# Moving lists, routing and layer-norm steps within the order of a gated attention and mixture-of-experts layer

## The chip, the cores and the metric

The kernel runs on one core of one Trainium2 chip. Its time is the device time of one execution in microseconds (us). A profile is taken from one execution by the hardware profiler; all instants are us from the start of its span. The engines are PE (matrix multiply, with its weight loads PEld), DVE (vector), ACT (scalar functions), POOL (general, here also the engine that issues indirect DMAs) and SP (which issues the other DMAs in the order of its queue).

## The reference

x is 8 batches of 512 tokens of 256 numbers, float32.

```python
x = x + tanh(g_xattn[0]) * xattn(layernorm(x), ctx, ctx, mask, ...)   # 16 heads of 16
x = x + tanh(g_ffn[0]) * ffn(layernorm(x), ...)

# ffn: 8 experts of 256 -> 1024 -> 256, two for each token
probs = softmax(x_flat @ router_w + router_b)
top_w, top_idx = top_k(probs, 2)
for e in range(8):
    out += comb[:, e:e+1] * (gelu(x_flat @ expert_up[e].T) @ expert_down[e].T)
```

All of this is computed in float32. Each of the 8 experts has 2 MB of weights. The mask is the same for all queries and heads and leaves a short run of keys, and the kernel finds that out on the chip and branches on it.

## The kernel before

**Ahead of the branch** (to about 19 us) the kernel loads the mask, the weights and x of batch 0, takes the statistics of batch 0's rows, finds the window of keys from the mask, and computes from it the flag `near_i` (L609), on which all engines branch (L1587). `measure` (L211) makes the layer norm's numbers: `look` runs BN_STATS and the aggregate for four tiles of 128 rows (L225, L228), and `settle` twelve small DVE operations that end in the scale and the shift (L233 to L246). Between the flag and the branch stand on DVE `drop` (L611, which reads the bank `row_ps` of a PE product), `pick`, `bks` and three `keep_ones` (L619). x of batch 1 is loaded behind the window load (L516), which waits on SP for the first key.

**Inside the branch** (`attend_near`) the attention of eight batches runs as one software pipeline. The outer loop's iteration b goes from -1 to 7. Each iteration has four groups g (a half c of the heads and an index i), and each group three slots n. A group of iteration b issues the attention weights of batch b (`weights_T`: `w_ps`, four products on PE with exponentials on ACT, L1058 and L1063), the product with the values of the group before (`weigh`: `n_av` on PE, then `raw`, its reciprocal, and `oT` on DVE, L1076 to L1090), the scores of batch b+1 (`find_tops`: `t_ps` on PE, the row maxima `tops` on DVE, L1028 and L1033), and `lower_tops` (`top_ps` on PE, `ql` on DVE, L1046 and L1047). All else is put in a plan of 12 places (g, n) by `between(old, new, next_)` with old = b-1, new = b+2 and next_ = b+3:

- for the new batch: keys and values (`kv_ps`, L539), `keys_T` (`k_ps`, with four ACT copies to `k`, L551 and L557), `keys_less` (`km`), the scales of its normalized rows (`xn_a` on ACT, L275), their transposes (`xnT_ps_a`, L285) and the two `queries` (`q_ps`, L570)
- for the next batch: the look and settle of its rows
- for the old batch: `project_out` in two halves (`proj_ps`, added to x on DVE, L1102), look and settle, the scales `xn_f`, the transposes, `logits` (`route_ps`), and then, one iteration later, the routing: `route` (a transpose `lg_ps`, L332, and some twenty small DVE operations with one exponential on ACT, which choose two experts for each token), `place` (`place_ps` on PE, `counts` on ACT, then POOL operations, which give each token a line in its expert's part of a table), and four steps `enter` of two indirect DMAs each, which write the table's entries (L398). `add_bias` runs on POOL for 2.35 us.

The banks of PSUM limit this order. The pool of scores has 5 banks, of which `t_ps` and `w_ps` take 4 each time; the pool "g" has 2, which `proj_ps`, `top_ps`, `lg_ps`, `kv_ps`, `k_ps`, `xnT_ps`, `q_ps`, `route_ps` and `place_ps` use in turn. PE takes its instructions in order, so it stands still where the next one's bank has not been read.

**The experts.** Tokens of one expert form groups of 256 (pairs) or 384 (triples). Of the 32 main groups 0 to 4 are planned when the first three batches are in the table (`plan_full(0)`), 5 to 16 when six are (`plan_full(1)`), and the others at the end (`plan_rest`). A group s needs its list of lines (`list_rows`, L806: SP reads the line number and loads 3 KB from the table), its rows (`fetch`, indirect DMAs on POOL, L826), its weights (`load`, L816 and L817, 1 MB each, three buffers), and then two products with GELU between them (L874, L892) and a scatter (L898). Groups 0 to 3 run between the attention groups of iterations 5 to 7 (the dictionary `amid`). From group 4 on `compute(s)` gives the steps of a group: fetch of s+2, the products, the turning of the next group's rows, the list of s+4, and the load of s+2. One step of the attention's last routing follows each of them: batches 6 and 7 are put into the table while groups 4 to 7 run. A list reads the table, so it waits for all entries that are issued ahead of it, and an entry waits for the reads ahead of it:

```python
            if s + 4 < end:
                steps.append(lambda: list_rows(s + 4))
            if s + 2 < end:
                steps.append(lambda: load(s + 2))
```

A framework puts the instructions of each engine in order by priority (that of the program) and by when its own model has the inputs ready, so an operation may slip ahead into a gap; `tc.keep_in_program_order` pins one to its place.

Of the kernel before, what the change touches and what calls it, by code (L numbers as in the profile page):

```python
# [68 lines left out]
def flamingo_layer(ctx: ExitStack, tc: tile.TileContext, a: dict, out: bass.AP):  # L69
# [190 lines left out]
    def shared(p2, small, bank):  # L260
        def layernorms(jobs, pin=False, measured=None):


            said, looks, settle_all = measured or measure(small, [job[:2] for job in jobs], pin)
            settle = lambda pin=False: settle_all(pin)

            def own(k):
                b, which, dst = jobs[k]

                def scale(ts):  # L270
                    if ts[0] == 0:
                        said[k] = p2.tile([P, QT, D], F32, tag="xn", name=f"xn_{which}_{b}")
                    for t in ts:
                        at = k * QT + t
                        ins = nc.scalar.activation(  # L275
                            said[k][:, t, :], xs[b][:, t, :], AF.Identity,
                            bias=said["shift"][:, at : at + 1], scale=said["rstd"][:, at : at + 1],
                        )
                        if t == ts[0] and pin:
                            tc.keep_in_program_order(ins)  # L280

                def turn(c):
                    ps = bank(f"xnT_ps_{which}_{b}_{c}")
                    for t in range(QT):
                        nc.tensor.transpose(ps[:, t * P : (t + 1) * P], said[k][:, t, c * P : (c + 1) * P], ident)  # L285
# [15 lines left out]
        def finish(b):  # L301
# [28 lines left out]
            def route():  # L330
                ps = bank(f"lg_ps{b}")[:, :P]
                nc.tensor.transpose(ps, said["lgT"], ident)  # L332
                lg = t3("lg")
                nc.vector.tensor_tensor(
                    lg, ps.rearrange("p (t e) -> p t e", t=QT)[:, :, :E], over_t(rb), ALU.add
                )
                mx = t2("mx")
                nc.vector.tensor_reduce(mx, lg, AX.X, ALU.max)
                nc.vector.tensor_tensor(lg, lg, over_e(mx), ALU.subtract)
                pr = t3("pr")  # L340
                nc.scalar.activation(pr, lg, AF.Exp)
                sm = t2("sm")
                nc.vector.tensor_reduce(sm, pr, AX.X, ALU.add)
                rs = t2("rs")
# [14 lines left out]
                both = t3("both")  # L359
                nc.vector.tensor_tensor(both, picks[:, :, 0, :], picks[:, :, 1, :], ALU.add)  # L360
                said["top"], said["picks"], said["both"] = top, picks, both
# [43 lines left out]
            return x2T, keep_x, keep_rows, logits, route, places  # L405

        return layernorms, finish

# [40 lines left out]
    with early, tc.tile_pool(name="ps_mask", bufs=1, space=PSUM) as ps_mask:  # L449
# [21 lines left out]
            ins = nc.vector.tensor_scalar(dropped[:, t, :], mask_i[:, t, :], 0.0, None, ALU.is_equal)  # L471
            tc.keep_in_program_order(ins)

        norms_0 = measure(const, [(0, "a")], True)
        settle_0 = norms_0[2]
        norms_0[1][0]()
        for t in range(QT):
# [35 lines left out]
            return t  # L513

        win = load_window(mk, 0)
        load_x(1, pin=True)  # L516
        wins = {1: load_window(const, 1, pin=True)}
        for dst, src in (
            (gates[:, 0:1], a["g_xattn"].partition_broadcast(P)),
# [87 lines left out]
        nc.vector.scalar_tensor_tensor(near, end, 1.0, near, ALU.is_ge, ALU.mult)  # L607
        nc.vector.scalar_tensor_tensor(near, uneven, 0.0, near, ALU.is_le, ALU.mult)
        tc.keep_in_program_order(nc.vector.tensor_copy(near_i, near))  # L609
        drop = column("drop", P)  # L610
        tc.keep_in_program_order(nc.vector.tensor_scalar(drop, row_ps, -1.0, 1.0, ALU.mult, ALU.add))  # L611
        nc.vector.scalar_tensor_tensor(pick, drop, lead, diag, ALU.mult, ALU.add)
# [6 lines left out]
            tc.keep_in_program_order(nc.vector.tensor_scalar(t[:, :, DH:], t[:, :, DH:], kept, None, ALU.mult))  # L619

        keep_ones(vals[0])
        for t in vals[1:]:
            keep_ones(t)
        for step in (keys_values, keys_T, lambda: stay_awake(6), keys_less):
# [4 lines left out]
    def experts(pool, seen, half_bank, bank, row_bank):  # L629
# [338 lines left out]
    def attend_near(att):  # L968
# [134 lines left out]

        normal = {}

        def normalize(*jobs):
            looks, settle, each = layernorms(jobs, True)
            for job, own in zip(jobs, each):
                normal[job[:2]] = own
            return looks, settle  # L1110

        def between(old, new, next_):
# [5 lines left out]
            def put(g, n, *steps):  # L1118
                plan[g, n] += steps

            jobs = []
            if old is not None:
                x2T, keep_x, keep_rows, logits, route, place = finish(old)
                jobs.append((old, "f", x2T))
            if next_ is not None:
                xnT[next_] = None
# [3 lines left out]
            if new is not None:  # L1130
# [18 lines left out]
                if new > 1:  # L1149
                    put(3, 0, bias)  # L1150
            if next_ is not None:
                put(*((2, 2) if old is None else (0, 2)), looks[-1])
            if old is not None:
                rows_f, scales, turns = normal[old, "f"]
                put(0, 1, lambda: project_out(old, (0, 1)))
                put(1, 0, lambda: project_out(old, (2, 3)), keep_x)
                put(1, 1, looks[0])
            if jobs:
                put(*((3, 1) if old is None else (1, 2)), settle)
            if old is not None:  # L1160
# [6 lines left out]
                later.append((route, place, enter, counts))  # L1167
            return plan


        def begin():
# [24 lines left out]
        DONE = 4  # L1196


        xnT, later = {}, deque()
        looks, settle = normalize((1, "a", lambda: xnT[1]))  # L1200
        for step in (*looks, settle):
            step()
        behind = None
        for b in range(-1, B):
            if b + 3 < B:
# [9 lines left out]
            if b == 0:  # L1215
                plan[0, 0] += looks
                plan[0, 1].insert(0, settle)
            for route, place, enter, counts in behind_route:
                plan[0, 2].append(route)
                plan[1, 2].append(place)  # L1220
                if counts:
                    plan[1, 2] += enter + counts
                else:
                    for where, step in zip(((1, 2), (2, 0), (2, 1), (2, 2)), enter):
                        plan[where].append(step)
            for g in range(4):
                c, i = g // 2, g % 2
# [20 lines left out]
        (route, place, enter, _), (route_last, last, enter_last, counts) = later  # L1248
        mixed = [step for pair in zip(rest, [route, place, *enter] + [wait] * len(rest)) for step in pair]
        spread = [step for one in enter_last for step in (one, wait, wait)]  # L1250
        queue = deque([*mixed, route_last, last, *spread, *counts])
# [12 lines left out]
    def attend_anywhere(att):  # L1264
# [141 lines left out]
            )  # L1406

        def end(b):
            x2T, keep_x, keep_rows, logits, route, place = finish(b)
            (look,), settle, ((normal, scales, turns),) = layernorms([(b, "f", x2T)])  # L1410
            return [keep_x, look, settle, *scales, lambda: keep_rows(normal()), *turns, logits, route, *place]

        def scores(b, h, t):
            q, kT, _ = qkv[b]
# [176 lines left out]
```

## Time and profile before

| | us |
|---|---|
| median of 5 runs | 793.22 (791.09 to 793.68) |
| the profiled execution | 791.3 |
| its span, first to last instruction | 789.5 |
| PE busy | 744.4 (94%) |
| DVE busy | 410.1 (52%) |
| ACT busy | 254.2 (32%) |
| POOL busy | 313.2 (40%) |
| mean granted clock of PE | 0.982 of full |

The profile consists of a page (busy times, the span in 40 slices, the chain that ended last, groups of instructions) and of answers to questions: the waits (which instruction stood still, by what it was released, the total, the times and the longest), the timeline (start, duration, engine, line, operation, output <- inputs, form, count, and in brackets the idle time of the engine ahead of it and what ended it), and windows (busy time of each engine in a stretch, the granted clock of PE, and the share and rate of the DMA engines). "SPq" is the queue of SP: its lines are issues of DMAs.

### The profile page before, as it was taken

Reading aid. Unit: us, or ns where it says so; the run is one execution under the profiler, and the core shown is the slowest. Engines: PE = TensorE matmul, PEld = TensorE weight load, DVE = VectorE, ACT = ScalarE, POOL = GpSimd, SP = SyncE. Lnnn points to the kernel's source line nnn. Section 1 sums busy time; section 2 is a strip of 40 time slices with the busy share of each in tenths; the row PEclk is TensorE's granted clock in tenths of the full one; section 3 lists DMA queues with packets and bytes.
Section 4 is the critical chain, followed back from the end, with each engine's and each line's share of the span. In section 5 each row is a group of like instructions: output and inputs, shape, how many; then the busy total and the mean of one; then the engine's idle time right before and its main releaser. Section 6 shows DMA issues by size and latency. Waiting matters only on the chain. (4 is left out here: it accounts for less than half of the span.)

```text
span 789.5 us, 11155 instructions
## 1 busy us (share of the span) xinstructions
PE 744.4 (94%) x3898; PEld 539.9 (68%) x3898; DVE 410.1 (52%) x1315; ACT 254.2 (32%) x487; POOL 313.2 (40%) x420
## 2 busy tenths in 40 slices
PE   8999989898999999998989999999999999999992
PEld 3544444443566666687868888888788788788872
DVE  7877888978756674352334443353533343333300
ACT  4564647456454353534111212111112211211110
POOL 2021106235456252655563444444343433444341
PEclk9998999999999999999999999999999999999996
DMA  5700211001853231245477757567546644754210
GB/s 166 273 8 8 81 34 58 29 30 57 278 192 116 94 104 53 81 150 158 142 250 245 251 177 232 196 210 230 167 167 213 208 160 156 244 180 169 101 48 25
DMA packets 82728, 113.32 MB, mean 144 GB/s; under 512 B 16605, under 2 KB 67552, under 8 KB 82656
## 3 DMA queue, kind: packets, MB, share of 16 engines
q1 hardware_dynamic: 70000, 85.16, 32.3%
q0 software_dynamic: 11840, 26.76, 10.3%
q8 instruction: 35, 0.57, 0.3%
q10 hardware_dynamic: 816, 0.53, 0.2%
q14 instruction: 37, 0.30, 0.1%
HBM read 92.66 MB, written 20.28 MB: 143 GB/s over the span
## 5 line engine op out<-in xcount | busy, mean ns | idle before, releaser
L874 PE MATMUL h_ps<-xT,up 128*128 128x256 f32 (+1 forms) x1024 | 244.4, 395 | 6.1 <-DMA up<-in_upT 6.1
L892 PE MATMUL o_ps<-down,hT 128*128 128x256 f32 x1088 | 242.5, 380 | 4.6 <-DVE y L895 4.6
L892 PEld LDWEIGHTS o_ps<-down,hT 128*128 128x128 f32 x1088 | 205.5, 190 | 39.7 <-DVE y L895 6.2
L874 PEld LDWEIGHTS h_ps<-xT,up 128*128 128x128 f32 x1024 | 194.2, 191 | 49.7 <-issue 7.0
L863 DVE STREAM_TRANSPOSE xT<-xg 32x128 f32<-32x128 f32 (+1 forms) x368 | 115.7, 314 | 182.1 <-DMA xg<-rows,listed 163.8
L878 ACT ACTIVATE hT<-h_ps 128x512 f32<-128x512 f32 (+1 forms) x144 | 82.2, 573 | 351.0 <-PE h_ps L874 351.0
L898 POOL DMA_INDIRECT out<-y,listed x68 | 68.6, 1008 | 145.7 <-DVE y L895 127.4
L826 POOL DMA_INDIRECT y<-out,listed x68 | 65.0, 956 | 79.2 <-DMA out<-y,listed 50.2
L1033 DVE TENSOR_REDUCE tops<-t_ps 128x4 f32<-128x512 f32 x128 | 79.2, 681 | 14.9 <-PE t_ps L1028 14.8
L826 POOL DMA_INDIRECT xg<-rows,listed x68 | 66.3, 975 | 39.9 <-issue 17.6
L1063 ACT ACTIVATE n_pT<-w_ps 128x512 f32<-128x512 f32 x128 | 67.3, 596 | 39.7 <-PE w_ps L1058 39.4
L398 POOL DMA_INDIRECT table<-entries,place_i x64 | 63.5, 992 | 24.0 <-issue 15.8
L895 DVE SCALAR_TENSOR_TENSOR y<-o_ps,listed,y 128x256 f32<-128x256 f32 x68 | 31.1, 481 | 73.4 <-PE o_ps L892 51.9
L1058 PE MATMUL w_ps<-ql,km 32*128 32x512 f32 x256 | 52.4, 655 | 2.0 <-DVE tops L1033 1.4
L1010 POOL TENSOR_TENSOR x<-x,bo 128x1024 f32<-128x1024 f32 x8 | 18.9, 2359 | 71.3 <-DVE bo L1009 42.0
L1028 PE MATMUL t_ps<-k,q 32*128 32x256 f32 x512 | 43.5, 411 | 1.1 <-ACT n_pT L1063 0.7
L1028 PEld LDWEIGHTS t_ps<-k,q 32*128 32x128 f32 x512 | 26.9, 188 | 21.5 <-issue 8.0
L1082 DVE STREAM_TRANSPOSE raw<-n_av 128x512 f32<-128x512 f32 x32 | 22.8, 712 | 28.5 <-PE n_av L1076 27.9
L1076 PE MATMUL n_av<-n_pT,nv 128*32 128x512 f32 x256 | 35.8, 633 | 1.2 <-DVE xT L851 1.1
L570 PE MATMUL q_ps<-n_xnT,wqT 128*128 128x512 f32 x64 | 31.4, 615 | 0.9 <-ACT n_xnT L286 0.6
L1097 PE MATMUL proj_ps<-woT,oT 128*128 128x256 f32 x128 | 31.5, 388 | 0.0
L1097 PEld LDWEIGHTS proj_ps<-woT,oT 128*128 128x128 f32 x128 | 23.4, 190 | 8.8 <-DVE mv_f_a L228 2.5
(220 smaller groups left out, 525.2 us busy)
## 6 DMA issues: line engine op xcount, KB each, us to landing
up<-in_upT SPq DMA_DIRECT2D x32, 1024.0 KB, 7.4
down<-in_downT SPq DMA_DIRECT2D x32, 1024.0 KB, 5.5
out<-x SPq DMA_DIRECT2D x8, 512.0 KB, 2.9
rows<-xn_f SPq DMA_DIRECT2D x8, 512.0 KB, 3.0
x<-in_x SPq DMA_DIRECT2D x7, 512.0 KB, 5.7
table<-none SPq DMA_DIRECT2D x1, 2400.0 KB, 12.8
xg<-rows,listed POOLq DMA_INDIRECT x68, 4.5
y<-out,listed POOLq DMA_INDIRECT x68, 2.7
```

Of the source, the lines that this page charges most:

```text
L398: nc.gpsimd.indirect_dma_start(out=table_parts[2 * t + i][:, :], out_offset=bass.IndirectOffsetOnAxis(ap=place_i[:, t, i : i + 1], axis=0) ...
L826: ins = nc.gpsimd.indirect_dma_start(out=dst, out_offset=None, in_=src[: seen[JOBS[s][0]], :], in_offset=bass.IndirectOffsetOnAxis(ap=list ...
L863: nc.vector.transpose(dst[32 * g : 32 * g + 32, i], src[32 * i : 32 * i + 32, g])
L874: nc.tensor.matmul(ps[:, i, :], lhsT=up[:, dc, (f + i) * P : (f + i + 1) * P], rhs=xT[:, dc, :], start=(dc == 0), stop=(dc == DC - 1),)
L878: nc.scalar.activation(made[s][:, f : f + m, :], ps, AF.Gelu)
L892: nc.tensor.matmul(ps, lhsT=hT[:, f, h * P : (h + 1) * P], rhs=down[:, f, :], start=(f == 0), stop=(f == FC - 1))
L898: ins = nc.gpsimd.indirect_dma_start(out=out_parts[h][:, :], out_offset=bass.IndirectOffsetOnAxis(ap=listed[:, n, h, 0:1], axis=0), in_=y[ ...
L1028: ins = nc.tensor.matmul(ps[j][:, u], lhsT=q[rows_j, c, t * P : (t + 1) * P], rhs=k[rows_j, c], start=True, stop=True)
L1033: nc.vector.tensor_reduce(top[:, 2 * tp : 2 * tp + 2, :].rearrange("p t (i x) -> p t i x", i=2)[:, :, :, 32 * j], ps[j], AX.X, ALU.max,)
L1058: ins = nc.tensor.matmul(ps[j], lhsT=km[rows_j, c, i, :], rhs=lowered[b, c][rows_j, i, :], start=True, stop=True)
L1063: nc.scalar.activation(pT[:, j, :], ps[j], AF.Exp)
L1097: nc.tensor.matmul(ps[:, t - ts[0], :], lhsT=outs[b, c][:, t * P : (t + 1) * P], rhs=w["woT"][:, c, :], start=(c == 0), stop=(c == DC - 1),)
```

## The change

1. `compute` takes a bound `listed`; the main loop passes LISTED = 17, so groups below 17 are not listed there. The lists of groups 6 to 16 are issued in one step at the end of iteration 7, group 3, where those of 6 and 7 were.
2. `route` is cut in two: `route` (the transpose and the addition that reads its bank) and `choose` (all the rest, its first operation pinned). For batches that no plan follows (0, 1, 3, 4) `route` goes from (0, 2) to (0, 0), `choose` to (1, 2), `place` from (1, 2) to (2, 2), and the entries from (1, 2) to (2, 2) on to (2, 2) to (3, 2). For the others both stay at (0, 2).
3. `keys_T` goes from (1, 1) to (1, 2) in iterations 0 to 5.
4. In iteration 0 the look of batch 3 goes from (2, 2) to (1, 2) and its settle from (3, 1) to (2, 0).
5. x of batch 1 is loaded ahead of the window load on SP, its look stands behind `near_i` and its settle behind the first `keep_ones`, all ahead of the branch.
6. Each of the four scale operations of a layer norm is pinned, where only the first of each two was.

```diff
-                        if t == ts[0] and pin:
+                        if pin:
                             tc.keep_in_program_order(ins)
...
             def route():
                 ps = bank(f"lg_ps{b}")[:, :P]
                 nc.tensor.transpose(ps, said["lgT"], ident)
-                lg = t3("lg")
+                said["lg"] = t3("lg")
                 nc.vector.tensor_tensor(
-                    lg, ps.rearrange("p (t e) -> p t e", t=QT)[:, :, :E], over_t(rb), ALU.add
-                )
+                    said["lg"], ps.rearrange("p (t e) -> p t e", t=QT)[:, :, :E], over_t(rb), ALU.add
+                )
+
+            def choose():
+                lg = said["lg"]
                 mx = t2("mx")
-                nc.vector.tensor_reduce(mx, lg, AX.X, ALU.max)
+                tc.keep_in_program_order(nc.vector.tensor_reduce(mx, lg, AX.X, ALU.max))
...
-        norms_0 = measure(const, [(0, "a")], True)
+        load_x(1, pin=True)
+        norms_0, norms_1 = (measure(const, [(b, "a")], True) for b in range(2))
...
         win = load_window(mk, 0)
-        load_x(1, pin=True)
...
         tc.keep_in_program_order(nc.vector.tensor_copy(near_i, near))
+        norms_1[1][0]()
...
         keep_ones(vals[0])
+        norms_1[2](True)
...
-        def compute(s, end, first):
+        def compute(s, end, first, listed=0):
...
-            if s + 4 < end:
+            if listed <= s + 4 < end:
                 steps.append(lambda: list_rows(s + 4))
...
-                    put(1, 1, *turns, keys_T)
+                    put(1, 1, *turns)
+                    put(1, 2, keys_T)
...
-                put(*((2, 2) if old is None else (0, 2)), looks[-1])
+                put(*((1, 2) if old is None else (0, 2)), looks[-1])
...
-                put(*((3, 1) if old is None else (1, 2)), settle)
+                put(*((2, 0) if old is None else (1, 2)), settle)
...
-            + [lambda: load(5), lambda: turn_rows(4), lambda: list_rows(6), lambda: list_rows(7)],
+            + [lambda: load(5), lambda: turn_rows(4), lambda: [list_rows(s) for s in range(6, LISTED)]],
...
-        looks, settle = normalize((1, "a", lambda: xnT[1]))
-        for step in (*looks, settle):
-            step()
+        normalize((1, "a", lambda: xnT[1]), measured=norms_1)
...
-            for route, place, enter, counts in behind_route:
-                plan[0, 2].append(route)
-                plan[1, 2].append(place)
+            for route, choose, place, enter, counts in behind_route:
                 if counts:
-                    plan[1, 2] += enter + counts
+                    plan[0, 2] += [route, choose]
+                    plan[1, 2] += [place, *enter, *counts]
                 else:
-                    for where, step in zip(((1, 2), (2, 0), (2, 1), (2, 2)), enter):
+                    plan[0, 0].append(route)
+                    plan[1, 2].append(choose)
+                    for where, step in zip(((2, 2), (2, 2), (3, 0), (3, 1), (3, 2)), (place, *enter)):
                         plan[where].append(step)
...
-            for step in compute(s, MAIN, DONE):
+            for step in compute(s, MAIN, DONE, LISTED):
```

More of the change, by code (lines that the diff above doesn't have):

```diff
@@ L404, in finish @@
             places = [place] + [lambda t=t: enter(t) for t in range(b * QT, (b + 1) * QT)]
-            return x2T, keep_x, keep_rows, logits, route, places
+            return x2T, keep_x, keep_rows, logits, route, choose, places
         return layernorms, finish
@@ L1104, in attend_near, with normalize @@
         normal = {}
-        def normalize(*jobs):
-            looks, settle, each = layernorms(jobs, True)
+        def normalize(*jobs, measured=None):
+            looks, settle, each = layernorms(jobs, True, measured)
             for job, own in zip(jobs, each):
@@ L1122, in between @@
             if old is not None:
-                x2T, keep_x, keep_rows, logits, route, place = finish(old)
+                x2T, keep_x, keep_rows, logits, route, choose, place = finish(old)
                 jobs.append((old, "f", x2T))
@@ L1166, in between @@
                 counts = [count for count, end in zip(plans, PARTS) if old + 1 == end]
-                later.append((route, place, enter, counts))
+                later.append((route, choose, place, enter, counts))
             return plan
@@ L1193, in attend_near @@
             (7, 3): [lambda: list_rows(5), lambda: fetch(5)] + downs(3)
[L1194 removed]
+            + [lambda: load(5), lambda: turn_rows(4), lambda: [list_rows(s) for s in range(6, LISTED)]],
         }
         DONE = 4
+        LISTED = SIZES[0] + SIZES[1]
         xnT, later = {}, deque()
[L1200 to L1202 removed]
+        normalize((1, "a", lambda: xnT[1]), measured=norms_1)
         behind = None
@@ L1247, in attend_near, with choice @@
         wait = lambda: None
-        (route, place, enter, _), (route_last, last, enter_last, counts) = later
-        mixed = [step for pair in zip(rest, [route, place, *enter] + [wait] * len(rest)) for step in pair]
+        (route, choose, place, enter, _), (route_last, choose_last, last, enter_last, counts) = later
+        def choice(route, choose):
+            route()
+            choose()
+        first = [lambda: choice(route, choose), place, *enter]
+        mixed = [step for pair in zip(rest, first + [wait] * len(rest)) for step in pair]
         spread = [step for one in enter_last for step in (one, wait, wait)]
-        queue = deque([*mixed, route_last, last, *spread, *counts])
+        queue = deque([*mixed, lambda: choice(route_last, choose_last), last, *spread, *counts])
         for s in range(DONE, MAIN):
-            for step in compute(s, MAIN, DONE):
+            for step in compute(s, MAIN, DONE, LISTED):
                 step()
@@ L1408, in end @@
         def end(b):
-            x2T, keep_x, keep_rows, logits, route, place = finish(b)
+            x2T, keep_x, keep_rows, logits, route, choose, place = finish(b)
             (look,), settle, ((normal, scales, turns),) = layernorms([(b, "f", x2T)])
-            return [keep_x, look, settle, *scales, lambda: keep_rows(normal()), *turns, logits, route, *place]
+            return [keep_x, look, settle, *scales, lambda: keep_rows(normal()), *turns, logits, route, choose, *place]
         def scores(b, h, t):
```

## The prediction

> **What bounds the kernel now.** I read the page first, then the waits of PE and of SP, then the timelines of PE, DVE and SP around each PE wait, with the clock by windows of 2 us. On the page PE is busy 744.4 of 789.5 us, DVE 52%, ACT 32%, POOL 40%. From about 200 us, where expert groups run between the attention steps, the PE slices are full but for a few, and after 416 us nearly all are; there only less PE work or a removed PE wait counts. Before 200 us PE and DVE hand tiles to each other: DVE is busy 15 to 18 of every 20 us. So I look for what ends PE's idle time. The waits of PE, longest first:
>
> ```profile
> PE h_ps L874 <- DMA up<-in_upT: 6.1, 2, 3.9
> PE o_ps L892 <- DVE y L895: 4.6, 4, 1.6
> PE xnT_ps_a L285 <- DVE x L1102: 3.5, 3, 1.2
> PE lg_ps L332 <- DVE x L1102: 2.8, 4, 0.9
> PE place_ps L368 <- ACT k L557: 2.3, 3, 0.8
> PE w_ps L1058 <- DVE tops L1033: 1.4, 1, 1.4
> ```
>
> The columns are total us, times, longest. The first is a transfer; the third to fifth are PSUM banks of the pool that rotates two (L285, L332, L368); the last is a score bank. The change touches all of these but the second.
>
> **Lists of the middle groups.** In the SP timeline a list (L806) stands right ahead of a weight load, and it waits for the table writes of batches 6 and 7:
>
> ```profile
> 359.75 0.37 SPq L806 DMA_DIRECT2D listed<-table  x1
> 360.69 0.37 SPq L816 DMA_DIRECT2D up<-in_upT  x1
> ...
> 396.61 0.37 SPq L806 DMA_DIRECT2D listed<-table  x1
> 397.72 0.37 SPq L816 DMA_DIRECT2D up<-in_upT  x1
> ```
>
> SP's waits say the same: L806 behind "table" 61.8 us in 12 waits, the longest 21.0. The weights of 360.69 land at 365.55, 2.13 us after PE wanted them, and those of 397.72 at 402.59:
>
> ```profile
> 391.45 7.21 PE L892 MATMUL o_ps<-down,hT 128*128 128x256 f32 x32 [0.86 <-DVE y L895]
> 402.59 8.59 PE L874 MATMUL h_ps<-xT,up 128*128 128x256 f32 x32 [3.94 <-DMA up<-in_upT]
> ```
>
> After the second gap the same 32 matmuls take 8.59 us, not 7.07 as at 383.08, and the clock reads 0.53 and 0.62 from 402 to 406: 1.5 us more. The new code issues lists 6 to 16 in one step where 6 and 7 stood (332.78). Two took 1.24 us there, so nine more take 9 x 0.87 = 7.8 us of SP, which issued nothing until 348.71: no cost. Batch 6's first table write, 356.16, must follow their reads; issued by 342, at the row's 4.7 us to landing they are in by 347. Then load(6) goes out behind the issue of 348.71, 11 us earlier, and later loads wait only for their buffers (L817 behind o_ps), which is how it runs after 419 anyway. What is late next: the rows for that group are transposed by 396.4, before PE comes to it at 398.65. So 2.1 + 3.9 + 1.5 = **7.5 us**. Bounds: 0 (the loads find another blocker) to 8.4 (POOL's two waits for a list, 4.0 us, also go and free the 0.86 above).
>
> **Batch 1 measured ahead of the branch.** Its DVE work inside the branch is four BN_STATS with aggregates (18.79 to 20.41) and 12 settle operations (21.80 to 24.14); the first row maximum follows at 24.06 although PE's scores are there from 21.65. Now the statistics stand behind near_i (15.91) and fill DVE's 1.23 us wait for row_ps; 1.6 us of them push `drop` from 17.15 to 17.55, and `pick` ends at 18.25, before PE needs it at 19.29. Then bks and one keep_ones to 18.8, settle (2.34) to 21.1, two keep_ones to 21.7. The 1.10 us that DVE waited at 21.51 (shown as DMA rw) ends at 21.5 by the old issue times, so it is covered. Row maxima start at about 22.1 instead of 24.06, ACT's xn_a at 22.5 instead of 24.23, and PE's next scores, 24.64, find their banks; DVE runs without a gap from there to 35, so **1.9 us** arrive. Bounds 0.8 (two stages of 1.1 if the wait for rw comes behind) to 2.2. The x load leaves SP at about 6 instead of 13.42; only wqT (needed at 13.19) and wkv (16.95) are on the way then, landed by 10.3. At the 5.7 us of such loads, x is there by 12. Cost nothing; without that cover, a late wqT would cost up to 1 us.
>
> **Batch 3 measured earlier (iteration 0).** Its statistics and settle ran from 58.53 to 62.65, ahead of `raw` and the row maxima (64.00), and PE stood still for their banks:
>
> ```profile
> 62.18 1.12 PE L1058 MATMUL w_ps<-ql,km 32*128 32x512 f32 x2
> 64.74 3.26 PE L1058 MATMUL w_ps<-ql,km 32*128 32x512 f32 x6 [1.44 <-DVE tops L1033]
> 67.93 1.94 PE L1076 MATMUL n_av<-n_pT,nv 128*32 128x512 f32 x8
> 69.80 2.57 PE L539 MATMUL kv_ps<-wkv,win 128*128 128x512 f32 x4
> ```
>
> The granted clock explains the long ones; windows of 2 us, the clock being the third number from the end:
>
> ```profile
> 62.00:64.00 2.00, 1.30 (x5) 0.30 (x3) 1.83 (x8) 1.31 (x3) 0.00 (x0) 1.00 0.00 0
> 64.00:66.00 2.00, 1.26 (x4) 1.06 (x5) 2.00 (x6) 0.75 (x2) 1.78 (x1) 0.55 0.00 0
> 66.00:68.00 2.00, 2.00 (x9) 0.50 (x10) 1.13 (x2) 1.15 (x2) 0.56 (x1) 0.50 0.03 8
> ```
>
> Against 1.14, 1.07 and 1.98 us elsewhere for w_ps, n_av and kv_ps, the half clock costs 2.4 + 0.9 + 0.6 = 3.9; with the gap 5.3. In their new place, group 1 slot 2 and group 2 slot 0, the 4.1 us of DVE work meet 1.35 + 0.69 us of DVE idle time (before 52.49 and 55.43), so the row maxima of group 2 come 2.06 us later, and I let PE pay that in full. 5.3 - 2.0 = **3.3 us**. Bounds 0 (a new half-clock stretch of 3.9) to 5.3.
>
> [...]
>
> **Route and choose in iterations 2 and 3.** PE waits 0.79 (lg_ps, 106.43), 1.18 (xnT_ps_a, 113.59) and 0.84 (place_ps, 116.42). The first goes, because the transpose moves to where no project_out is in front. The second goes, because DVE has the 3.0 us of the choice (108.66 to 111.55, and both at 112.11) ahead of `x` at 112.85; without it `x` is done by 110.7, and PE asks at 111.3. The third moves behind q_ps and may come back as 0 to 1 us. PE gains up to 2.8 per iteration. But DVE gets the 3.0 us back at slot (1,2), ahead of the row maxima of group 2, which therefore start again at 122.75; what stays is DVE's idle time in group 3 (0.25 + 1.37 + 0.49 = 2.1), of which PE's lead removes part. I take half of 2.8, **1.4 us each, 2.8 together**; bounds 0 and 5.6. On POOL, place and the eight table writes (14 us) come 8 us later, with add_bias (2.35 us) after the first two; x with bias is needed at 139.3, 3.5 us after it ended in the old order; if all eight writes stood ahead of it, PE would lose 3 us.
>
> **The rest.** keys_T behind lower_tops frees 0.24 us in iteration 1: 0.2. In iteration 4 (which keeps its route at 0,2) place_ps then gets a bank that DVE's ql frees at 185.0, not ACT's k at 183.2: between a gain of 1.2 and a loss of 1.5, I take a loss of **0.5**. The pins on every scale move three xn_a (1.58 us) from ACT's busy stretch at 124.30 to its 4.43 us idle at 103: no cost, gain 0 to 0.7 (the wait at 191.58), taken as 0. Iterations 5 and 6: PE has only one such wait, 0.4 at 211: **0.4**. The tail after 750 us is untouched.
>
> **Sum.** 7.5 + 1.9 + 3.3 + 2.8 + 0.2 + 0.4 - 0.5 = 15.6 us. The profiled execution had a span of 789.5 and took 791.3 us, so it would take 775.7. The median of the runs shown, 793.2, lies 1.9 above it, and I subtract from that: 777.6, said as **778**.
>
> **Rivals.** (A) As above, 772 to 782: chance 0.52. (B) The attention part is bound by DVE, whose work hardly shrinks, so that only the lists and the start pay: 793.2 - 9.4 = 784; for it speaks DVE's 1.9 of 2 us between 178 and 192. 0.25. (C) The loads meet another blocker, and only attention gains 8.1: 785; against it, SP's free time from 333 to 348. 0.10. (D) Slower: the choice in front of the row maxima of group 2 makes PE wait and starts half-clock stretches as at 64 and 194 to 201 us. One costs 4.3 (3.9 there, 4.7 by the four groups at 192) plus a gap of 1.4. With one each in iterations 0, 2, 3, 5 and 6 it is 5 x 5.7 = 28.5 against 15.6 + 5.3 - 3.3 (iteration 0's new one is in the count): 793.2 + 11 = 804; from four on it is slower than before. 0.07. (E) Eleven lists at once fill the queue, as one list did at 204 us (5.15 us of issue); from 2.5 us each, load(6) would leave later than now (332.8 + 11 x 2.5 = 360.3); at 5.15 it leaves 29 us later, and 793.2 + 29 - 8 = 814. Against it, two lists behind 2 MB took 1.24 us. 0.02. (F) The planner, which is free to move what isn't pinned, puts things back: within 0.2% of 793. 0.04.
>
> **Numbers.** A measurement of this kernel can tell 0.2%, 1.6 us. Faster: A, B, C, 0.87; same 0.04; slower 0.09. The range 770 to 789 takes in A to C with their bounds and leaves out D to F and the ends.
>
> **What would show it.** Right: no PE wait for `up` near 363 and 400; eleven L806 in a row near 333 us and none in SP's way until group 13; row maxima from about 22; full clock from 62 to 72; no lg_ps and xnT_ps_a waits in iterations 2 and 3. Wrong: a new wait of w_ps on the row maxima in groups 2 and 3 with a clock of 0.5, or `up` still late, behind another SP wait.

## The result, and the profile after

The changed kernel takes 792.4 us (median of 29 runs, 789.9 to 797.3), the kernel before, run beside it, 792.0 (51 runs): ratio 1.0007, 95% interval 0.9999 to 1.0015. No difference can be measured; the forecast was 778. The profiled execution has a span of 793.5 us and a mean clock of 0.976, where before had 789.5 and 0.982. Where "lost clock" is given below, it is one minus the granted clock, summed over the length of a stretch: 2 us at half clock lose 1 us.

The waits of PE in the changed kernel (total us, times, longest), to be held against those of before:

```profile
PE o_ps L897 <- DVE y L900: 10.3, 5, 5.9
PE place_ps L371 <- DVE both L363: 6.2, 4, 2.8
PE x_ps L854 <- DMA xg<-rows,listed: 2.0, 1, 2.0
PE place_ps L371 <- ACT k L560: 1.6, 1, 1.6
...
PE xnT_ps_a L285 <- DVE x L1107: 1.2, 1, 1.2
...
PE lg_ps L332 <- DVE x L1107: 1.0, 1, 1.0
```

What the change aimed at is gone: no wait for `up` (was 6.1 us), none of w_ps for `tops` (1.4), and 1.2 and 1.0 where xnT_ps_a and lg_ps lost 3.5 and 2.8. But o_ps waits 10.3 where it waited 4.6, place_ps 6.2 behind `both` where it waited 0.8, and x_ps's 2.0 behind the first group's rows are new.

**Where the time went** shows in instants. Iteration 2 starts 5.9 us earlier than before (91.66 against 97.51) and iteration 3 is 7.7 ahead (123.69). The lead is 5.8 at iteration 5 (196.39), 3.0 at iteration 6 (258.32), and then becomes a lag: iteration 7 starts at 301.92, 3.1 late, and the group behind 421 us is 3.5 late, as are all later ones. Three places take it. The first is the new place of the routing; PE and DVE in iteration 3:

```profile
146.52 0.60 PE L1051 MATMUL top_ps<-ident,tops 128*128 128x128 f32 x4
148.69 0.38 PE L371 MATMUL place_ps<-both,before 128*128 128x32 f32 x2 [1.57 <-DVE both L363]
...
149.23 3.03 PE L1063 MATMUL w_ps<-ql,km 32*128 32x512 f32 x8
```

```profile
148.35 0.19 DVE L363 TENSOR_TENSOR both<-picks 128x32 f32<-128x32 f32 x1
148.46 2.48 DVE L1038 TENSOR_REDUCE tops<-t_ps 128x4 f32<-128x512 f32 x4
```

PE waits for the last operation of the choice, and only then do the row maxima of group 2 start. The w_ps behind place_ps, which need those maxima done, are drawn out too: in iteration 2, at full clock, the eight take 2.29 us (117.21), where in before they took 1.14 (116.96). The windows (clock third from the end) show what follows in iteration 3, 3.4 us of clock lost from 150 to 158:

```profile
152.00:154.00 2.00, 2.00 (x9) 0.20 (x8) 0.00 (x0) 1.41 (x4) 1.42 (x6) 0.50 0.00 0
```

Iteration 2 has the same wait (1.57) with no lost clock behind it, iteration 6 one of 2.81 with another 3.4 us of clock from 280 to 288.

The second place is the first group's rows. Their fetch leaves 2.7 us earlier than before (199.51 against 202.24), less than PE is ahead, so x_ps waits 2.05 us for them at 206.88, and 1.7 us of clock are lost from 208 to 213.

The third place is where the lists were to pay. PE, then POOL and DVE, in the changed kernel:

```profile
399.09 7.07 PE L879 MATMUL h_ps<-xT,up 128*128 128x256 f32 x32
412.02 9.56 PE L897 MATMUL o_ps<-down,hT 128*128 128x256 f32 x32 [5.86 <-DVE y L900]
421.42 2.75 PE L879 MATMUL h_ps<-xT,up 128*128 128x256 f32 x12
```

```profile
397.15 0.96 POOL L401 DMA_INDIRECT table<-entries,place_i  x1 [0.30 <-issue]
398.42 1.00 POOL L903 DMA_INDIRECT out<-y,listed  x1 [0.30 <-issue]
399.72 0.96 POOL L401 DMA_INDIRECT table<-entries,place_i  x1 [0.30 <-issue]
400.98 0.96 POOL L401 DMA_INDIRECT table<-entries,place_i  x1 [0.30 <-issue]
402.25 0.99 POOL L903 DMA_INDIRECT out<-y,listed  x1 [0.30 <-issue]
408.64 0.99 POOL L831 DMA_INDIRECT y<-out,listed  x1 [5.40 <-issue]
```

```profile
394.93 0.48 DVE L900 SCALAR_TENSOR_TENSOR y<-o_ps,listed,y 128x256 f32<-128x256 f32 x1
411.48 0.48 DVE L900 SCALAR_TENSOR_TENSOR y<-o_ps,listed,y 128x256 f32<-128x256 f32 x1 [10.03 <-issue]
```

A group's result rows are added on DVE to rows of `out` that POOL has fetched, and scattered back; the next group's fetch of such rows waits until that scatter has landed. The second y of a group is ready at 395.4, but its scatter stands in POOL's queue behind eight table writes of batch 7 (390.71 to 401.94) and leaves at 402.25. The fetch follows 5.40 us after it, DVE can add at 411.48, and PE, whose product needs the bank that this addition reads, has waited 5.86 us. Half clock begins inside this wait, at 410, and lasts to 417 (9.56 us for 32 matmuls that take 7.07). The profile names no releaser for this fetch ("issue"); that it is the landing is read from lists_paced below, where the same fetch waits 5.46 us and is put down to `DMA out<-y,listed`.

Before, the order in POOL's queue was another:

```profile
395.57 1.00 POOL L898 DMA_INDIRECT out<-y,listed  x1 [0.30 <-DVE far L694]
396.87 1.00 POOL L898 DMA_INDIRECT out<-y,listed  x1 [0.30 <-issue]
398.58 0.96 POOL L398 DMA_INDIRECT table<-entries,place_i  x1 [0.70 <-DMA listed<-table]
...
403.64 0.99 POOL L826 DMA_INDIRECT y<-out,listed  x1 [0.30 <-issue]
```

Both scatters left behind four of the eight table writes, and the other four were issued while they landed, so the fetch followed without a wait. The second y was ready at 394.88 and the addition ran at 406.44, 11.6 us later and before PE came at 411.02. In the changed kernel it is 395.41 to 411.48, 16.1 us. So the waits for `up` did not only stand in front of this chain: without the lists among the table writes the chain is 4.5 us longer. The runs below agree. With the lists in their old places and POOL's order left to the framework (no_lists, start_only, iter0_only) the order is that of before; with the lists in one step (lists_only, lists_paced, route_back) the second scatter stands behind all eight writes. The fifth write above waits for a list's read; why the framework chooses the other order without it isn't shown.

### The profile page after: what moved, and what is told of

Its sections match the earlier page's. It is cut to its first block, busy times and chain, and to the rows that moved or that the text cites. A ratio compares the mean times of both kernels' runs of the same rounds, so it can differ in the third digit from the quotient of the medians.

```text
span 793.5 us, 11153 instructions
## 1 busy us (share of the span) xinstructions
PE 745.5 (94%) x3898; PEld 542.7 (68%) x3898; DVE 410.3 (52%) x1315; ACT 257.7 (32%) x489; POOL 312.7 (39%) x420
## 5 line engine op out<-in xcount | busy, mean ns | idle before, releaser
L897 PE MATMUL o_ps<-down,hT 128*128 128x256 f32 x1088 | 244.9, 383 | 10.3 <-DVE y L900 10.3
L1063 PE MATMUL w_ps<-ql,km 32*128 32x512 f32 x256 | 56.0, 669 | 0.0
L1033 PE MATMUL t_ps<-k,q 32*128 32x256 f32 x512 | 39.3, 408 | 0.3 <-ACT k L560 0.3
L1081 PE MATMUL n_av<-n_pT,nv 128*32 128x512 f32 x256 | 37.5, 661 | 1.4 <-DVE xT L856 1.4
L1033 PEld LDWEIGHTS t_ps<-k,q 32*128 32x128 f32 x512 | 25.0, 188 | 16.9 <-issue 9.6
```

What stands on the lines that cost most here:

```text
L897: nc.tensor.matmul(ps, lhsT=hT[:, f, h * P : (h + 1) * P], rhs=down[:, f, :], start=(f == 0), stop=(f == FC - 1))
L1033: ins = nc.tensor.matmul(ps[j][:, u], lhsT=q[rows_j, c, t * P : (t + 1) * P], rhs=k[rows_j, c], start=True, stop=True)
L1063: ins = nc.tensor.matmul(ps[j], lhsT=km[rows_j, c, i, :], rhs=lowered[b, c][rows_j, i, :], start=True, stop=True)
```

## The experiments

Theory 1, formed from these traces: the waits for `up` were in front of others, so their 7.5 us go to the y chain on POOL; and the choice in its new slot makes PE wait and starts half-clock stretches. Theory 2 is the forecast: each wait that goes is time won. All times are medians of 4 to 12 executions, ratios to the kernel before on the same chip; each four rows of the table are from one chip.

| run | us | before | ratio (95%) |
|---|---|---|---|
| lists_only | 791.5 | 792.7 | 0.9989 (0.9976 to 1.0001) |
| lists_paced | 790.8 | 792.7 | 0.9973 (0.9955 to 0.9990) |
| route_back | 789.1 | 792.7 | 0.9961 (0.9944 to 0.9977) |
| no_lists | 793.8 | 792.7 | 1.0022 (1.0007 to 1.0038) |
| scatter_first | 783.9 | 792.2 | 0.9906 (0.9883 to 0.9928) |
| route_back_scatter | 781.9 | 792.2 | 0.9860 (0.9846 to 0.9875) |
| start_only | 791.1 | 792.2 | 0.9983 (0.9972 to 0.9993) |
| iter0_only | 788.4 | 792.2 | 0.9958 (0.9945 to 0.9972) |
| lists_scatter | 818.0 | 812.6 | 1.0063 (1.0046 to 1.0079) |
| scatter_only | 818.9 | 812.6 | 1.0066 (1.0045 to 1.0088) |
| place_later_scatter | 806.8 | 812.6 | 0.9920 (0.9892 to 0.9947) |
| keys_back | 809.3 | 812.6 | 0.9954 (0.9937 to 0.9972) |
| lists_scatter_b | 784.3 | 792.8 | 0.9891 (0.9874 to 0.9909) |
| scatter_only_b | 799.2 | 792.8 | 1.0084 (1.0065 to 1.0104) |
| place_later_b | 788.3 | 792.8 | 0.9950 (0.9932 to 0.9968) |
| keys_back_b | 777.6 | 792.8 | 0.9812 (0.9792 to 0.9833) |

**lists_only**: the kernel before with part 1 of the change.

```diff
-            if s + 4 < end:
+            if listed <= s + 4 < end:
                 steps.append(lambda: list_rows(s + 4))
...
-            + [lambda: load(5), lambda: turn_rows(4), lambda: list_rows(6), lambda: list_rows(7)],
+            + [lambda: load(5), lambda: turn_rows(4), lambda: [list_rows(s) for s in range(6, LISTED)]],
```

> The kernel before with the lists of groups 6 to 16 issued in one step, nothing else of the change. Theory 1 (the waits for up were in front of others): the loads are early, but the first result row of group 6 is scattered behind the table writes of batch 7 on POOL, the y rows come late, PE waits about 6 us for y near 410 us and runs at half clock behind it; nothing is won: 791 to 796 us, ratio 0.999 to 1.005. Theory 2 (the forecast: each removed wait is time won): 7.5 us less, 784.5 us, ratio 0.9905.

0.9 us less, and the interval reaches to nothing: theory 1. The waits for `up` are gone, and one stands in their place, o_ps 5.21 us behind y at 407.70, with 3.4 us of clock lost from 405 to 413. The second y is ready at 390.96 and the addition runs at 407.17, 16.2 us later, with the order of the changed kernel on POOL; with the 11.6 us of before it would have run at about 402.5 (an estimate), when PE came.

**lists_paced**: lists_only with an empty step where the list was, since each step of `compute` also takes one step of the routing queue.

```diff
-            if listed <= s + 4 < end:
-                steps.append(lambda: list_rows(s + 4))
+            if s + 4 < end:
+                steps.append(lambda: list_rows(s + 4) if s + 4 >= listed else None)
```

> As lists_only, but where a list step stood an empty step stands, so that the queue of routing steps is taken at the old pace and batch 7's table writes keep their place among the groups. Theory 1: one table write fewer stands in front of the first scatter of group 6, and the scatter is back to about the old time; most of the 7.5 us comes: 784 to 787 us. Theory 2: 784.5, the same as lists_only. A third theory (the pace isn't it; a blocker of another kind follows the lists): 791 to 796 us, as lists_only.

A miss: one table write fewer stands ahead of the first scatter (five, not six), but the second leaves at 398.00, as in lists_only (397.79), and PE waits 5.44 us. 790.8 is not told apart from 791.5. The pace of the queue isn't the cause. What is left is that the eight writes stand ahead of the second scatter at all, which scatter_first tests.

**no_lists**: the changed kernel with part 1 undone (the diff of lists_only backwards).

> The changed kernel with the lists back in their old places, all else changed. Theory 1: the lists give nothing in this kernel, so taking them back costs nothing or wins up to 3 us: 789 to 793 us, and PE starts the groups behind 420 us no later. Theory 2: 7.5 us more, 800 us, with the waits for up of 2.1 and 3.9 us back.

1.5 parts in a thousand, 1.2 us, slower than the changed kernel, 0.8 us above the range of theory 1 and far from theory 2. The waits for `up` are back and larger (5.99 us at 368.40, 2.06 at 404.81), since PE came to them earlier, with half clock from 366, inside the first, to 374. The order on POOL is again that of before, and the long wait for y is gone. One of the two chains costs about what the other does.

**scatter_first**: the changed kernel; batch 7's `place` comes ten steps later in the queue, and the scatter of group 6 and the table writes of batch 7 are pinned to their place in the program, as the scatters of the later groups are already. POOL's order becomes scatter, two writes, scatter, two fetches of rows, two writes, two fetches of y, four writes.

```diff
-            in_turn(s + 1, ins)
+            in_turn(s + 2, ins)
...
+                    if b == B - 1 and near:
+                        tc.keep_in_program_order(ins)
...
-        queue = deque([*mixed, lambda: choice(route_last, choose_last), last, *spread, *counts])
+        queue = deque([*mixed, lambda: choice(route_last, choose_last), *[wait] * 10, last, *spread, *counts])
```

> The changed kernel with the first result rows of group 6 scattered ahead of most of batch 7's table writes on POOL (batch 7's place step ten steps later, and the order of its table writes kept as written), nothing else. Theory 1 (the list gain is taken by the chain scatter, landing, y fetch on POOL): PE's wait of 5.9 us for y near 412 us and the half clock of 410 to 417 us (3.4 us of clock) go, 6 to 9 us less than the changed kernel: 783 to 787 us. Theory 2 (the gain is lost elsewhere, the y chain would be late anyway by its own length): within 2 us of the changed kernel, 790 to 794 us, a wait for y of 4 us or more still there.

783.9, 1.0% below the changed kernel, as theory 1 has it. No wait for y near 412 is left; the longest of o_ps is 1.3, and place_ps, which now comes later, waits 1.8 for y at 386.56.

**lists_scatter and scatter_only**, on the kernel before: the scatter order with the lists of part 1, and without them.

> The kernel before with two things only: the lists of groups 6 to 16 in one step, and the first result rows of group 6 scattered ahead of most of batch 7's table writes (as in scatter_first). Theory 1 (the forecast's price of the lists holds once the y chain is out of the way): lists_only less its wait of 5.2 us for y and at least 1.7 us of clock, 783 to 786 us. Theory 2 (another blocker stands behind that one): 788 to 792 us.

> The kernel before with the scatter order alone, the lists in their old places. Theory 1 (neither half pays alone): the lists still stand in front of the weight loads on SP and now wait for table writes that end about 15 us later, so the waits for up stay or grow: 792 to 800 us. If the scatter order alone carries what scatter_first won: 784 to 787 us.

These two, place_later_scatter and keys_back ran on a chip where the kernel before takes 812.6 us. Its traces have pauses of PE without a releaser and one of ACT of 10.7 us (last section), so no theory is judged by them; in their own ratios lists_scatter and scatter_only are equally 0.6% slower than before, and why the pair loses there isn't shown (lg_ps waits 6.4 us for lgT there, which it doesn't in lists_scatter_b). All four were run again elsewhere:

> lists_scatter again, on a chip where the kernel before takes about 792 us. Theory 1 (the forecast's price of the lists holds once the y chain is out of the way): 783 to 786 us, ratio 0.990 to 0.993. Theory 2 (another blocker stands behind that one): 788 to 792 us, ratio 0.995 to 1.0.

> scatter_only again. Theory 1 (neither half pays alone: the lists still stand in front of the weight loads and wait for table writes that end later): 792 to 800 us, ratio 1.000 to 1.010. If the scatter order alone carries the gain: 784 to 787 us, ratio 0.990 to 0.994.

784.3 and 799.2: neither half pays alone, and both together win 8.6 us. In lists_scatter_b PE runs through where it waited before, here PE and then POOL:

```profile
394.81 7.07 PE L876 MATMUL h_ps<-xT,up 128*128 128x256 f32 x32
401.71 7.07 PE L894 MATMUL o_ps<-down,hT 128*128 128x256 f32 x32
408.62 7.07 PE L876 MATMUL h_ps<-xT,up 128*128 128x256 f32 x32
417.21 6.96 PE L894 MATMUL o_ps<-down,hT 128*128 128x256 f32 x31 [1.52 <-DVE y L897]
```

```profile
399.47 1.05 POOL L900 DMA_INDIRECT out<-y,listed  x1 [0.68 <-DVE before L661]
400.83 0.98 POOL L398 DMA_INDIRECT table<-entries,place_i  x1 [0.31 <-issue]
402.11 0.96 POOL L398 DMA_INDIRECT table<-entries,place_i  x1 [0.30 <-issue]
403.38 0.99 POOL L900 DMA_INDIRECT out<-y,listed  x1 [0.30 <-DVE extra L792]
```

In scatter_only_b the lists are back on SP and wait for table writes that end later: a list leaves at 413.84, the load behind it at 414.92, and PE waits 3.11 us for `up` at 420.13. So the forecast's 7.5 us for the lists were there, but only together with an order on POOL that lets the scatters leave early; left to itself, that order got worse when the lists went.

**route_back and route_back_scatter**: the changed kernel, and scatter_first, with route, choose, place and entries in the slots of before.

```diff
+                plan[0, 2] += [route, choose]
+                plan[1, 2].append(place)
...
-                    plan[0, 0].append(route)
-                    plan[1, 2].append(choose)
-                    for where, step in zip(((2, 2), (2, 2), (3, 0), (3, 1), (3, 2)), (place, *enter)):
+                    for where, step in zip(((1, 2), (2, 0), (2, 1), (2, 2)), enter):
                         plan[where].append(step)
```

> The changed kernel with route, choose, place and the bias steps of the batches in the slots they had before; all else changed. Theory 1: the choice directly ahead of both makes place_ps wait (1.57 us in iterations 2 and 3, 2.81 us in iteration 6) and starts half-clock stretches of about 3.4 us of clock each at 150 and 280 us; undoing it wins 1.6 + 3.4 for iteration 3 and 2.8 + 3.4 for iteration 6 and pays up to 2 us in iteration 2: 783 to 788 us, the stretches at 150 and 280 us gone. Theory 2 (the forecast): 2.8 us slower than the changed kernel, 795 us, with the waits of lg_ps and xnT_ps_a back in iterations 2 and 3.

> scatter_first with route, choose, place and the bias steps back in the slots of the kernel before. If the two losses (the choice ahead of both, and the y chain) are separate, their gains add: 789.1 less 6 to 9, 780 to 783 us. If they hide each other, 786 to 790 us.

route_back is 0.46% (3.6 us) faster than the changed kernel where the forecast said 2.8 slower (1.1 us above the range of theory 1), and no wait behind `both` of over 0.25 us is left; route_back_scatter is another 1.0% lower. The losses of the routing and of the y chain add up. The waits alone don't explain the 3.6 us: with those behind `both` gone, lg_ps waits 2.6 us again, xnT_ps_a 3.5 and place_ps 4.9 for k, against 1.0, 1.2 and 1.6, about as much as was won. The clock does: one minus the mean clock, times the span, averages 18.8 us over the executions of the changed kernel and 15.6 over those of route_back. On one chip it is 16.2 in scatter_first and 12.9 in route_back_scatter, which is all of their difference.

**place_later_scatter and place_later_b**: scatter_first with place and entries one slot later.

```diff
-                    for where, step in zip(((2, 2), (2, 2), (3, 0), (3, 1), (3, 2)), (place, *enter)):
+                    for where, step in zip(((3, 0), (3, 0), (3, 1), (3, 2), (3, 2)), (place, *enter)):
```

> scatter_first with place and the bias steps one slot later still (from group 2 slot 2 to group 3 slot 0). Theory 1a (the choice makes PE wait only because place_ps stands behind it): the waits for both (1.57, 1.58, 2.81 us) go and two half-clock stretches with them: 775 to 779 us. Theory 1b (the choice stands ahead of the row maxima too, so PE's scores w_ps wait for their banks instead): within 1.5 us of scatter_first, 782 to 786 us, with new waits of w_ps or n_av for tops in group 2.

> place_later_scatter again. Theory 1a (PE waits for the choice only through place_ps): ratio 0.978 to 0.984 of before, 775 to 779 us. Theory 1b (the choice stands ahead of the row maxima, PE's scores wait for their banks instead, as 1.03 us at 117 and 2.31 us at 291 us in the run on the other chip): within 1.5 us of scatter_first, ratio 0.989 to 0.993, 782 to 786 us.

The mechanism is that of 1b, the rival (D) of the prediction: place_ps no longer waits for `both`, and w_ps waits for its score banks. PE in iteration 6 of place_later_b:

```profile
277.14 2.67 PE L1065 MATMUL w_ps<-ql,km 32*128 32x512 f32 x5 [2.31 <-DVE tops L1040]
```

In iterations 2 and 3 it waits 1.03 and 1.04. Half clock follows two of the three. The time, 788.3, is 2 us above what 1b gave; the profiled run's span is only 1.5 us above that of scatter_first, so this rest stays open.

**start_only and iter0_only**: parts 5 and 4 of the change alone, on the kernel before.

> The kernel before with the load, statistics and settling of batch 1 ahead of the branch, nothing else. Theory 1 (DVE's lead of 1 us is lost again where PE and DVE hand tiles over, and by 62 us PE is 1.3 earlier, which is carried on to the end): 791.4 us, ratio 0.998. Theory 2 (the forecast): 1.9 us less, 790.8 us. A third (a later wait takes it): 792.7 us, ratio 1.000.

> The kernel before with the look and settle of iteration 0 at the earlier slots, nothing else. Theory 1 (as read in the changed kernel, where iteration 1 starts 1.3 and iteration 2 5.9 us earlier): 4.5 us less at the start of iteration 2, half clock of 64 to 71 us gone, and as later stages keep most of the lead, 788 to 790 us. Theory 2 (the forecast): 3.3 us less, 789.4 us. A third (PE's lead is eaten before 421 us by the chain table writes, lists, first rows): 792 to 793 us, the lead gone at the first x_ps.

1.3 us (0.6 to 2.2 by the interval) and 3.3 (2.2 to 4.4). In iter0_only the gap of 1.44 us at 64 us is gone and with it the half clock behind: n_av and kv_ps run at full speed and iteration 2 starts at 93.84, not 97.51. Over all executions the lost clock is 11.7 us on average, 14.6 in before beside it: 2.9 of the 3.3. Both carry to the end, unlike the lists. The first wait for `up` is only 0.2 us longer (2.36).

**keys_back and keys_back_b**: route_back_scatter with part 3 undone.

```diff
-                    put(1, 1, *turns)
-                    put(1, 2, keys_T)
+                    put(1, 1, *turns, keys_T)
```

> route_back_scatter with keys_T back at group 1 slot 1 in all iterations. Theory 1 (place_ps gets its bank later because k is copied later): the waits of place_ps for k in iterations 2 to 4 fall from 1.69, 1.60, 1.60 to 0.84, 0.75, 0.75 us: 2.5 us less, 779 to 780 us. Rival (PE's next wait, t_ps or top_ps in the same iterations, takes it): 781 to 782.5 us.

> keys_back again: route_back_scatter (781.9 us, ratio 0.986) with keys_T back at group 1 slot 1. Theory 1 (place_ps gets its bank later because k is copied later): 2.5 us less, 779.4 us, ratio 0.983. Rival (the next wait takes it): ratio 0.985 to 0.987.

777.6 us: 1.9% faster than before, and the fastest of all. The same instruction of iteration 2, first in route_back_scatter, then in keys_back_b:

```profile
111.68 0.38 PE L371 MATMUL place_ps<-both,before 128*128 128x32 f32 x2 [1.69 <-ACT k L562]
```

```profile
110.68 0.38 PE L371 MATMUL place_ps<-both,before 128*128 128x32 f32 x2 [0.85 <-ACT k L562]
```

ACT's four copies to `k` end 1.0 us later where keys_T comes later, and place_ps takes the bank that they free. By ratio part 3 costs 0.48% (3.8 us), more than the 2.5 us of waits: in route_back_scatter each of the three waits is followed by 1.7 us of lost clock, in keys_back_b none is (its one stretch, of 3.4 us, begins at 188, behind no wait of more than 0.2 us). Over all executions, four and five of them, the lost clock averages 12.9 and 9.0 us, as much as the whole difference; so what became of the 2.5 us of waits beside it stays open.

## Why the prediction was wrong, point by point

- **Lists, 7.5 us: the mechanism right, the size lost.** No wait for `up`, eleven lists in a row from 336.28, load(6) out at 348.67, as forecast (the lists took 11.83 us, not 1.24 + 7.8, in time that cost nothing). The step that failed is "What is late next: the rows for that group are transposed by 396.4, before PE comes to it at 398.65". I looked at xT, one input, and not at the other: o_ps needs DVE's addition, which needs the y fetch, the scatter, and POOL's queue. The forecast's own words, "later loads wait only for their buffers [...], which is how it runs after 419 anyway", took a steady state for a stretch in which POOL also writes a batch into the table. It also took the order on POOL as given: it changed with the lists, and the way from the second y to the next addition went from 11.6 to 16.1 us. Alone the lists gave 0.9 us; with the scatter order 8.6 (7.2 to 10.0).
- **Batch 1 ahead of the branch, 1.9: right in kind, 1.3 measured** (within its bounds of 0.8 to 2.2; the interval, 0.6 to 2.2, doesn't exclude 1.9). The row maxima start at 22.82, not 22.1: DVE was ready, and waited 0.90 us for `t_ps`. I had taken the scores as there from 21.65, which is where their 1.15 us begin.
- **Iteration 0, 3.3: right, 3.3 measured.** The terms were each a little off and made up for it: the stretch at 64 lost 3.4 us of clock, not 3.9, and the lead at iteration 2 (3.7 us of the 1.44 + 3.4) shows that PE paid 1.2, not 2.0, for the new place.
- **Route and choose, 2.8 gained (and 0.4 for iterations 5 and 6): wrong in sign, a loss of 3.6.** The step is "DVE gets the 3.0 us back at slot (1,2), ahead of the row maxima of group 2 [...] PE's lead removes part. I take half". The lg_ps and xnT_ps_a waits did go. But DVE's work only changed its place in front of PE: place_ps waited 1.57, 1.57 and 2.81 us, not "0 to 1", and place_later_b showed that without place_ps w_ps waits there instead. The waits came out about even, and the clock lost behind them, 3.2 us more on average, which the step put at nothing, made the loss. The bounds, 0 and 5.6, had no loss in them though rival (D) described it.
- **keys_T, 0.2 gained and 0.5 lost: wrong.** "place_ps then gets a bank that DVE's ql frees at 185.0, not ACT's k": it still waited for k, 1.60 us, with 1.7 us of clock behind.
- **The sum.** Measured alone or by undoing: 0.9 + 1.3 + 3.3 gained, 3.6 lost to the routing, and by one trace 0.85 + 1.7 to keys_T in iteration 4: 0.7 us slower in all, against 0.5 (-0.1 to 1.2) measured. That the sum closes so well is in part luck: each measured part is uncertain by about 1 us, the clock lost behind a wait varies (last section), and the pins of part 6 were not measured alone. The base of 793.2 was also 1.3 us above the median of 51 executions. But the nought is a balance of gains and losses, not a change without effect. Rival (F), which named 793, isn't what happened: the loads and the choice did move, though the framework did reorder POOL. Of (C) its price came true, the lists won next to nothing, but the loads were in time and PE met the blocker. (D) came true in iterations 3 and 6, two stretches and not its five.

## What to carry to other kernels

When a wait goes, follow every input of the next instructions to its own chain and queue, not only the one that is easy to see: the 7.5 us existed, and it took a scatter ahead of six of eight table writes in one queue to get them. Where a framework orders a queue, check that a moved step has not changed the order of others in it. Where two engines hand tiles over without slack, moving work of the full one from in front of one of PE's instructions to in front of another won nothing here; look for what stands behind the new place. A change of several parts that comes out at nought is worth taking apart: leaving out two of its parts and adding the scatter order gives 777.6 us.

## What the runs showed of the hardware

The half-clock stretches ahead of the end of PE's work, summed in 1-us windows, lost 3.42, 3.41 and 1.71 us of clock in the kernel before (from 64, 193 and 402 us) and 3.42, 1.70, 1.71, 3.41 and 3.42 in the changed kernel (from 150, 181, 208, 280 and 410). Stretches began inside or right behind recorded waits of 1.04 us (place_later_b, 150), 1.44 (before, 64), 1.57 and 1.60 (the changed kernel, 150 and 181), and one of 3.42 us (keys_back_b, 188) behind none of over 0.2. The length of a wait did not settle in these runs whether a stretch followed. The wait of place_ps behind `both` in iterations 2 and 3, 1.57 or 1.58 us in the changed kernel, no_lists and scatter_first, was followed by no lost clock twice, by 1.7 us twice and by 3.4 us twice; waits of 1.18 or 1.19 us (xnT_ps_a in the kernel before, three times) by none.

One chip was slower in its own way: before took 812.6 us there, 2.6% more. PE and ACT in keys_back on it:

```profile
391.81 0.48 PE L332 MATMUL lg_ps<-ident,lgT 128*128 128x128 f32 x1 [8.15 <-ACT lgT L328]
```

```profile
391.49 0.27 ACT L328 COPY lgT<-route_ps 128x128 f32<-128x128 f32 x1 [10.67 <-remote]
```

In keys_back_b lg_ps of the same batch came without a wait, at 364.42. PE, too, had pauses of 1 to 1.7 us ahead of route_ps and h_ps that no wait explains. What held them isn't in the trace and stays open, so times from that chip are not held against the others here.
